# Two neighbouring transformer blocks on one core: a later place for two position tables, and a deeper ring for the first pass over the MLP weights

## The chip, the cores and the metric

The kernel runs on one core of one Trainium2 chip. The time is device microseconds (us) of the program, as the median of several runs. Five engines take their instructions in order, each from a queue of its own: PE (matrix products), DVE (vector), ACT (scalar functions), POOL (GpSimd) and SP, which here only issues DMA transfers. They wait for each other through semaphores. What decides the time is how long PE, which has nearly all the work, stands idle or runs at a lower granted clock.

## The reference

A sequence of 32 x 64 rows of 512 numbers goes through two blocks. Cut to what matters:

```python
# block 0: rotary attention with 8 heads over one key/value head, then a gated MLP
h = x * rsqrt(mean(x**2) + 1e-6) * (w * (1 + t @ tw.T))
q, k, v = h @ Wq.T, h @ Wk.T, h @ Wv.T           # 8 heads of 64, one k and v
q, k = rope(q, pos_ids), rope(k, pos_ids)        # cos and sin of pos * inv_freq
x = x + softmax(q k^T / 8) v @ Wo.T
h = ada_rms(x)                                   # second weights
x = x + (silu(h @ Wg.T) * (h @ Wu.T)) @ Wd.T     # 512 -> 2048 -> 512
# block 1: LayerNorm with scale and shift from t, keys and values through a latent of 128
h = layernorm(x) * (1 + scale) + shift
k, v = (h @ Wkd.T) @ Wku.T, (h @ Wkd.T) @ Wvu.T  # 16 heads, 4 k/v heads, rope
x = x + softmax(mask(q k^T / sqrt(32))) v @ Wo.T
```

The positions are an input, so the cosines and sines of block 0 are computed on the chip; that is what `angles` does.

## The kernel before, in words

All arithmetic is in 32-bit floats. The 2048 rows are cut into eight units of 256 (`NU`, `UT`). `attention0(u)` is the first block's attention of a unit, `attention1(u)` the second block's, and `mlp(j)` the first block's MLP for a block of units: `BLOCKS = ((0,), (1, 2), (3, 4), (5, 6), (7,))`, so mlp(0) is the MLP of unit 0, mlp(1) that of units 1 and 2, and so on. Each `mlp(j)` is one pass over all MLP weights.

**The order of the work.** PE's order is written by a planner at build time: jobs (the MLP pass, the attention of the units that the next pass needs, the second block's attention of units that are done) are generators that yield costs, and class `Order` (L74) takes the next piece from the job that is least advanced. The stretch before mlp(0), the prelude, has its order written out by hand in `FIRST`, with unit 0's attention ("a"), unit 1's ("b") and the four modulations ("m"). While mlp(0) runs (about 61 to 178 us), unit 2's attention is worked in; during mlp(1), units 3 and 4; during mlp(2), units 5 and 6; during mlp(3), unit 7 (`in_turn`, L1277). The other engines' queues follow from the order in which the code issues their instructions and from the build's own ordering of what has no dependence.

**The angles.** `angles(u0)` (L410 to L452) computes the cosines and sines for the two units u0 and u0 + 1 at once: 35 DVE instructions on 128 x 128 tiles (a cast L423; sign and size L424 to L427; splitting L428 to L430; products L438, rounding L433 and L434, sums L444 to L446) and two Sin on ACT (L450, L451), with a last DVE product L452. It is called through the argument `late` at the end of an `attention0`. `angles(2)` is called in the prelude and runs from 99 to 122 us. `angles(4)` is called at the end of unit 2's attention and `angles(6)` at the end of unit 4's. Who reads the result is the first step of an `attention0`: `tab` (L491), eight matmuls that turn the tables into the layout of q and k, from which DVE makes `cs` (L500). Unit 4's tab stands at 278.4 us and unit 6's at 527.9.

**The weights.** A pass has 24 weight sets: three matrices (gate, up, down) by eight groups q of 256 columns. In a pass they come as two halves of four groups, each eight gate and up sets and then four down sets. A product is done with seven block products in place of eight (P1 to P7): EARLIER (P1, P6, P5, P7) reads the f part of a set, four tiles, and LATER (P2, P3, P4) reads the l part, three tiles. Four of the seven tiles are sums of quarters of the matrix. In the first pass the four raw quarters of a set are loaded (two to l, one to f, one to a tile `a`, here called a21), and `sums_of_set` (L325) makes the sums: L330, L331, L332 on DVE (on POOL for sets 0 and 1), L333 on POOL. The sums are stored to memory (`kept`) by `done_with`, and the later passes load them ready made.

**The ring.** The sets live in `MW = 4` slots of each kind. When PE is done with a part of set n, `done_with` (L335) issues the load of set n + 4: in the first pass, all of it at once, when the l part is done (`load_sets`, L304); later each part by itself (`load_part`, L288). The a21 tile has two buffers (L310). `combine` (L317) issues the sums up to two sets ahead of PE's use; for sets 2 to 4 they are held back behind a mark in DVE's queue (L322), so that they don't stand ahead of the prelude's work. `other_mods` (L1187) loads sets 2 and 3 after the second modulation.

**The elementwise part of the MLP.** ACT copies a product out (e, L1059), DVE adds (L1060, L1061, L1080, L1089, L1098), ACT does silu (L1092), POOL the gating (L1100 to L1103), and PE takes the down products (`gu` and `down` both at L1044). In attention, DVE turns q (L631 to L633), takes the softmax's maximum, difference, sum and reciprocal (L643, L644, L651, L652), POOL scales (p, L653), PE transposes (pp, L658), ACT copies (pT, L659), and DVE adds the result (po) to x at L679.

Of the kernel before, what the change touches and what calls it, by code (L numbers as in the profile page):

```python
# [17 lines left out]
P = 128  # L18
# [5 lines left out]
NU = T // UT  # L24
HT = UT // 2
FF = 2048
NP = FF // P // 2
# [103 lines left out]
def two_blocks(ctx: ExitStack, tc: tile.TileContext, a: dict, out: bass.AP):  # L131
# [44 lines left out]
    def fixed(shape):  # L176
        n, i = int(np.prod(shape[1:])), stays["at"]
        stays["at"] += n
        assert stays["at"] <= STAY
        t = stays["all"][:, i : i + n]  # L180
        if len(shape) == 2:
            return t
        names = "abc"[: len(shape) - 1]
        return t.rearrange(f"p ({' '.join(names)}) -> p {' '.join(names)}", **dict(zip(names, shape[1:])))

    def work(tag, shape, name, bufs=2):
        return wk.tile(shape, F32, tag=tag, name=name, bufs=bufs)
# [81 lines left out]
        x_units[u] = xt  # L269


    MW = 4
    EARLIER = ("P1", "P6", "P5", "P7")
    LATER = ("P2", "P3", "P4")
    OF = {"P1": ("f", 3, "B11"), "P6": ("f", 1, "T2"), "P5": ("f", 0, "T1"), "P7": ("f", 2, "T3")}
# [7 lines left out]
    sets, odd = {"f": {}, "l": {}}, {}  # L283

    slots = {kind: [fixed([P, parts, 2 * P]) for i in range(MW)] for kind, parts in (("f", 4), ("l", 3))}
    act_slots = [fixed([P, 7, 2 * HT]) for i in GROUPS[0]]

    def load_part(kind, n):  # L288
        if n >= len(sequence) or n in sets[kind]:
            return  # L290
        j, m, q = sequence[n]
        i = 3 * q + m
        t = slots[kind][n % MW]
        if kind == "f":
            nc.sync.dma_start(t[:, 3], a["wmlp"][i][:, 0])
            if j:
                nc.sync.dma_start(t[:, 0:3], kept[i][:, 0:3])
        else:
            nc.sync.dma_start(t[:, 0:2], a["wmlp"][i][:, 1:3])
            if j:  # L300
                nc.sync.dma_start(t[:, 2], kept[i][:, 3])
        sets[kind][n] = t

    def load_sets(upto):  # L304
        for n in range(upto):
            if n in odd:
                continue
            load_part("f", n)
            load_part("l", n)
            odd[n] = work("a21", [P, 2 * P], f"a21_{n}", 2)  # L310
            nc.sync.dma_start(odd[n], a["wmlp"][3 * sequence[n][2] + sequence[n][1]][:, 3])

    marks, roots = [], []
# [21 lines left out]
    def done_with(kind, what):  # L335
        n = place[what]
        j, m, q = what
        if j == 0:
            to = kept[3 * q + m]
            if kind == "l":  # L340
                nc.sync.dma_start(to[:, 3], sets["l"][n][:, 2])
            else:
                nc.sync.dma_start(to[:, 0:3], sets["f"][n][:, 0:3])
        if n + MW < 3 * NP:
            if kind == "l":
                load_sets(n + MW + 1)
        else:
            load_part(kind, n + MW)

    mods = []  # L350

# [835 lines left out]
    def other_mods():  # L1187
        for i in range(1, 4):
            yield from modulation(i)
            if i == 1:  # L1190
                load_sets(MW)

    def second(u, room=None):
        room = room or {"ring": "1"}
# [11 lines left out]
    for _ in modulation(0):  # L1206
        pass
    load_positions(2)
    load_sets(2)
    load_mod(2)  # L1210
    load_mod(3)
# [7 lines left out]
    ahead = Job(attention0(1, {"ring": "1", "lean": True}, late=later_angles), A0)  # L1219
# [57 lines left out]
    def in_turn(units):  # L1277
        for u in units:
            while u not in x_units or u not in turned_units:
                yield 0.0, 1.0  # L1280
            late = (lambda u=u: angles(u + 2)) if u % 2 == 0 and u + 2 < NU else None
            yield from attention0(u, {"ring": "0"}, late=late)

    chain = Job(behind(), 0.8 * A1)
    for j, units in enumerate(BLOCKS):
# [5 lines left out]
        if j + 1 < len(BLOCKS):  # L1291
            more = [u for u in BLOCKS[j + 1] if u > 1]
# [112 lines left out]
```

## Time and profile before

| what | value |
| --- | --- |
| median of 3 runs | 1021.75 us (1021.2 to 1022.19) |
| profiled execution | 1023.49 us, span 1021.7 us |
| PE busy | 987.5 us, 97% of the span |
| DVE, ACT, POOL busy | 543.4, 302.9, 423.1 us |
| PE busy from 50 to 200 us | 136.1 of 150 us |
| DVE busy from 100 to 150 us | 43.97 of 50 us |
| mean granted clock of PE | 0.992 |

The profile is one execution; its parts are the engines' busy times, the span in 40 slices, the chain of waits that ended last, groups of instructions by line, and the DMA transfers. In a row of the timeline stand the start, the length, the engine, the line, the operation with output and inputs, and in brackets the idle time before it and what ended it. PE's idle time is what a change of order can win or lose: an engine that is not the bound may be idle for nothing. A PE instruction that waits on DVE or POOL has everything behind it in PE's queue waiting too.

### The profile page before, as it was taken

Reading aid. Unit: us, or ns where it says so; the run is one execution under the profiler, and the core shown is the slowest. Engines: PE = TensorE matmul, PEld = TensorE weight load, DVE = VectorE, ACT = ScalarE, POOL = GpSimd, SP = SyncE. Lnnn points to the kernel's source line nnn. Section 1 sums busy time; section 2 is a strip of 40 time slices with the busy share of each in tenths; the row PEclk is TensorE's granted clock in tenths of the full one; section 3 lists DMA queues with packets and bytes.
Section 4 is the critical chain, followed back from the end, with each engine's and each line's share of the span. In section 5 each row is a group of like instructions: output and inputs, shape, how many; then the busy total and the mean of one; then the engine's idle time right before and its main releaser. Section 6 shows DMA issues by size and latency. Waiting matters only on the chain.

```text
span 1021.7 us, 17480 instructions
## 1 busy us (share of the span) xinstructions
PE 987.5 (97%) x6710; PEld 857.6 (84%) x6710; DVE 543.4 (53%) x1188; ACT 302.9 (30%) x552; POOL 423.1 (41%) x439
## 2 busy tenths in 40 slices
PE   8999897999999999999999999999999989999998
PEld 7788887988877888888788887888788868998986
DVE  4757898654386442644446362455424632645274
ACT  4433142323215310225313351222313320425032
POOL 4336255354522433444344333554325432853252
PEclk9999998999999999999999999999999999999999
DMA  7927753724222345323242233333233424847301
GB/s 265 320 95 250 228 165 123 242 62 138 76 68 73 108 134 181 109 72 105 78 129 78 73 119 125 123 104 109 84 99 113 124 93 139 261 145 223 101 2 42
DMA packets 82642, 132.23 MB, mean 129 GB/s; under 512 B 8832, under 2 KB 48512, under 8 KB 82176
## 3 DMA queue, kind: packets, MB, share of 16 engines
q1 hardware_dynamic: 82560, 131.12, 40.1%
q8 instruction: 53, 0.87, 0.4%
q14 instruction: 29, 0.24, 0.1%
HBM read 114.31 MB, written 16.78 MB: 128 GB/s over the span
## 4 chain that ended last, share of the span: by engine, by line
PE 84%; DVE 8%; POOL 2%; DMA 2%; issue 2%; ACT 1%; POOLq 0%; SPq 0%; DVEq 0%; ACTq 0%
PE gu L1044 36%; PE down L1044 16%; PE q L623 11%; PE po L623 10%; PE sc L973 2%; PE pp L658 2%; PE kv L623 1%; PE lat L623 1%; PE cx L1003 1%; DMA stays<-in_wmlp 1%; PE cx L802 1%; ACT cT L812 1%; PE sc L781 1%; PE tab L491 1%; DVE mx L643 1%
## 5 line engine op out<-in xcount | busy, mean ns | idle before, releaser
L1044 PE MATMUL gu<-h,stays 128*128 128x256 f32 (+1 forms) x1280 | 261.2, 342 | 9.6 <-ACT gate L1092 5.8
L1044 PEld LDWEIGHTS gu<-h,stays 128*128 128x128 f32 x1280 | 208.4, 192 | 35.2 <-ACT gate L1092 6.0
L1044 PE MATMUL down<-stays 128*128 128x256 f32 (+1 forms) x1120 | 211.6, 344 | 2.0 <-DVE u_d L1060 2.0
L1044 PEld LDWEIGHTS down<-stays 128*128 128x128 f32 x1120 | 180.0, 194 | 25.9 <-issue 5.2
L1044 PE MATMUL gu<-hc,stays 128*128 128x256 f32 (+1 forms) x960 | 195.6, 339 | 0.5 <-DVE stays L331 0.5
L1044 PEld LDWEIGHTS gu<-hc,stays 128*128 128x128 f32 x960 | 157.9, 192 | 16.0 <-DVE stays L331 0.6
L623 PE MATMUL q<-h,stays 128*128 128x256 f32 x480 | 109.5, 381 | 0.0
L623 PE MATMUL po<-cT,stays 128*128 128x256 f32 x480 | 107.7, 381 | 0.9 <-ACT cT L812 0.7
L623 PEld LDWEIGHTS po<-cT,stays 128*128 128x128 f32 x480 | 90.4, 190 | 13.9 <-ACT cT L812 1.8
L623 PEld LDWEIGHTS q<-h,stays 128*128 128x128 f32 x480 | 90.6, 191 | 11.9 <-issue 0.2
L1100 POOL TENSOR_TENSOR stays<-gate,stays 128x768 f32<-128x768 f32 (+1 forms) x40 | 53.5, 1337 | 109.3 <-DVE stays L1089 102.4
L1059 ACT COPY e<-gu 128x256 f32<-128x256 f32 (+1 forms) x80 | 26.1, 326 | 193.9 <-PE gu L1044 193.8
L653 POOL TENSOR_TENSOR p<-p,sm 128x512 f32<-128x512 f32 x40 | 41.5, 1055 | 93.6 <-DVE sm L652 90.1
L634 POOL TENSOR_TENSOR qT<-u_q,v_q 128x512 f32<-128x512 f32 x30 | 38.1, 1268 | 90.0 <-DVE v_q L633 83.4
L679 DVE TENSOR_TENSOR x<-x,po 128x512 f32<-128x512 f32 x28 | 19.2, 687 | 99.2 <-PE po L623 99.2
L1060 DVE TENSOR_TENSOR u<-e,gu 128x256 f32<-128x256 f32 (+1 forms) x80 | 28.7, 360 | 61.1 <-ACT e L1059 61.1
L610 POOL TENSOR_TENSOR h<-x,stays 128x1024 f32<-128x1024 f32 x12 | 23.0, 1916 | 68.9 <-DVE x L679 51.2
L1061 DVE TENSOR_TENSOR w<-u,gu 128x256 f32<-128x256 f32 (+1 forms) x80 | 29.2, 365 | 30.9 <-PE gu L1044 30.0
L1101 POOL TENSOR_TENSOR stays<-stays 128x512 f32<-128x512 f32 (+1 forms) x40 | 43.8, 1096 | 2.7 <-DVE posf L423 0.2
L565 DVE RECIPROCAL stays<-stays 128x256 f32<-128x256 f32 (+1 forms) x23 | 35.4, 1540 | 16.9 <-ACT stays L564 16.8
L1147 POOL TENSOR_TENSOR x<-x,c 128x256 f32<-128x256 f32 x16 | 12.0, 749 | 74.8 <-DVE c L1134 74.8
L643 DVE TENSOR_REDUCE mx<-sc 128x8 f32<-128x512 f32 (+1 forms) x52 | 31.4, 641 | 17.6 <-PE sc L973 15.3
(233 smaller groups left out, 1281.9 us busy)
## 6 DMA issues: line engine op xcount, KB each, us to landing
stays<-sums SPq DMA_DIRECT2D x96, 384.0 KB, 3.1
stays<-in_wmlp SPq DMA_DIRECT2D x120, 256.0 KB, 3.1
stays<-in_wmlp SPq DMA_DIRECT2D x120, 128.0 KB, 2.6
stays<-sums SPq DMA_DIRECT2D x96, 128.0 KB, 2.4
sums<-stays SPq DMA_DIRECT2D x24, 384.0 KB, 3.7
mod<-in_mod SPq DMA_DIRECT2D x8, 512.0 KB, 5.4
x<-in_x SPq DMA_DIRECT2D x8, 512.0 KB, 5.6
a<-in_wmlp SPq DMA_DIRECT2D x24, 128.0 KB, 3.4
```

What stands on the lines that cost most here:

```text
L565: nc.vector.reciprocal(r, r)
L610: nc.gpsimd.tensor_tensor(by_seq(h), by_seq(x), per_seq(s, u), ALU.mult)
L623: nc.tensor.matmul(ps, w[:, k, cols], h[:, k, :], start=(k == 0), stop=(k == KC - 1))
L634: nc.gpsimd.tensor_tensor(dst, u, v, ALU.add)
L643: nc.vector.tensor_reduce(mx, s3, AX.X, ALU.max)
L653: nc.gpsimd.tensor_tensor(p8, p8, sm.unsqueeze(2).to_broadcast(wide), ALU.mult)
L1044: nc.tensor.matmul(ps[REGION[p]][:, c], w[:, slot, cols], moving, start=opening and ps.opens(p, c, k), stop=p in LATER, skip_group_check=True,
L1059: nc.scalar.copy(e, ps[0])
L1060: nc.vector.tensor_tensor(u2, e, ps[1], ALU.add)
L1061: nc.vector.tensor_tensor(w2, u2, ps[2], ALU.add)
L1100: e.tensor_tensor(act[:, 2:5], gate[:, 1:4], act[:, 2:5], ALU.mult)
L1101: e.tensor_tensor(act[:, 0:4:2], act[:, 2:4], act[:, 1:3], ALU.subtract)
```

## The change

Two things are changed, and nothing of the arithmetic.

1. `FIRST_MW = 6`: in the first pass the ring has six slots. The two extra slots (`more`) are tiles of the working pool. A set's load is issued when the set six before it is done. The a21 tile gets four buffers. `other_mods` loads sets 2 to 5 after the second modulation. In the first pass the slots of the sets 22 and 23 are not loaded again, and the second pass's first four sets are loaded when sets 18 to 21 are done. From the second pass on the ring has four slots, as before.
2. `late` now belongs to the odd units: unit 3's attention ends with `angles(4)` and unit 5's with `angles(6)`. So angles(4) moves from mlp(0) to mlp(1), directly ahead of unit 4's attention, and angles(6) from mlp(1) to mlp(2), directly ahead of unit 6's. `angles(2)` stays.

```diff
-    MW = 4
+    MW, FIRST_MW = 4, 6
...
     slots = {kind: [fixed([P, parts, 2 * P]) for i in range(MW)] for kind, parts in (("f", 4), ("l", 3))}
+    for i in range(FIRST_MW - MW):
+        t = work("more", [P, 7, 2 * P], f"more_{i}", FIRST_MW - MW)
+        slots["f"].append(t[:, 0:4])
+        slots["l"].append(t[:, 4:7])
...
-        t = slots[kind][n % MW]
+        t = slots[kind][n % (MW if j else FIRST_MW)]
...
-            odd[n] = work("a21", [P, 2 * P], f"a21_{n}", 2)
+            odd[n] = work("a21", [P, 2 * P], f"a21_{n}", 4)
...
-        if n + MW < 3 * NP:
+        ahead = n + (MW if j else FIRST_MW)
+        if ahead < 3 * NP:
             if kind == "l":
-                load_sets(n + MW + 1)
-        else:
-            load_part(kind, n + MW)
+                load_sets(ahead + 1)
+        elif j or n < 3 * NP - FIRST_MW + MW:
+            load_part(kind, ahead)
...
             if i == 1:
-                load_sets(MW)
+                load_sets(FIRST_MW)
...
-            late = (lambda u=u: angles(u + 2)) if u % 2 == 0 and u + 2 < NU else None
+            late = (lambda u=u: angles(u + 1)) if u % 2 and u + 1 < NU else None
```

In the order of PE's queue this moves a few matmuls of mlp(0), and in mlp(1) it puts 28 down products ahead of unit 4's tab that stood behind it; from there on PE's order is the same as before. On DVE the instructions of the two angles move with their calls, and set 5's sums stand in the prelude.

## The prediction

> **What bounds the kernel now.** I read the page's first two parts, then PE's busy time by stretches, then the list of what PE waited for, and last the timeline of two gaps.
>
> The page: busy time per engine, and the clock granted to PE in 40 slices.
>
> ```profile
> span 1021.7 us, 17480 instructions
> PE 987.5 (97%) x6710; PEld 857.6 (84%) x6710; DVE 543.4 (53%) x1188; ACT 302.9 (30%) x552; POOL 423.1 (41%) x439
> ...
> PEclk9999998999999999999999999999999999999999
> ```
>
> PE is the bound. The change leaves its matmuls alone, so all it can win or lose is PE's 34 us of idle time and the stretches at a lower clock. Where they lie shows in the busy time by stretches (us; then PE, PEld, DVE, ACT, POOL busy; granted clock, DMA share, GB/s):
>
> ```profile
> 50.00:100.00 50.00, 46.67 (x439) 42.79 (x438) 31.10 (x81) 18.20 (x38) 22.61 (x29) 1.00 0.53 178
> 100.00:150.00 50.00, 45.27 (x386) 41.16 (x385) 43.97 (x118) 14.06 (x26) 20.31 (x26) 0.97 0.59 191
> 150.00:200.00 50.00, 44.16 (x288) 41.54 (x287) 36.71 (x82) 13.78 (x25) 22.64 (x26) 0.93 0.59 193
> 200.00:250.00 50.00, 50.00 (x293) 43.65 (x292) 28.58 (x58) 13.62 (x22) 23.70 (x19) 1.00 0.32 99
> ...
> 300.00:400.00 100.00, 96.97 (x515) 81.75 (x510) 49.93 (x100) 25.91 (x45) 34.29 (x32) 1.00 0.38 120
> 400.00:500.00 100.00, 99.98 (x613) 85.13 (x611) 51.70 (x102) 33.64 (x55) 49.18 (x45) 1.00 0.32 97
> ```
>
> Some 14 us are idle between 50 and 200 us, which is the first pass over the weights (mlp(0), about 61 to 178 us). 3 us are idle in the second pass (300 to 400), nothing in the third (400 to 500). What ended PE's waits from 60 to 210 us (total, times, longest):
>
> ```profile
> PE gu L1044 <- ACT gate L1092: 5.8, 1, 5.8
> PE down L1044 <- DVE u_d L1060: 2.0, 1, 2.0
> PE gu L1044 <- issue: 1.2, 2, 0.9
> PE gu L1044 <- ACT sq_a L597: 1.0, 1, 1.0
> ```
>
> The 5.8 us gap is one event. The timeline of its makers (start, length, [idle before]):
>
> ```profile
> 165.28 1.97 DVE L434 TENSOR_TENSOR stays<-stays 128x128 f32<-128x128 f32 x1
> ...
> 167.82 0.92 DVE L452 TENSOR_TENSOR stays<-stays,sign 128x128 f32<-128x128 f32 x1
> 168.66 1.48 DVE L330 TENSOR_TENSOR stays<-a,stays 128x256 f32<-128x256 f32 x1
> ...
> 171.76 0.29 DVE L1080 TENSOR_TENSOR stays<-w,gu 128x128 f32<-128x128 f32 x1
> ```
> ```profile
> 172.15 2.05 PE L1044 MATMUL gu<-h,stays 128*128 128x128 f32 x8 [5.84 <-ACT gate L1092]
> ```
>
> The last up products of group 7 wait for L1080 on DVE, which stands behind the last of angles(4) (L423 to L452, 15.5 us of DVE from 135 to 169 us) and two sums of weights. The eight matmuls then take 2.05 us, where the same eight at 159.63 took 1.05: the granted clock was 0.50 from 172 to 175 us.
>
> In the second pass angles(6) does the same on a smaller scale:
>
> ```profile
> 308.55 1.12 PE L1003 MATMUL cx<-pT,stays 64*32 64x256 f32 x16 [2.57 <-ACT pT L659]
> ```
>
> **The change, part by part** (in the profiled execution of before: 1023.49 us, span 1021.7, 1.8 outside it; it lies 1.7 above the median 1021.75, and I take the sum off either).
>
> *angles(4) leaves mlp(0).* 35 DVE instructions and two Sin. L1080 then needs e (L1059), which needs sq_b and sq_a on ACT (1.06 and 1.04) after the second L679. Unit 2's po ends at 159.6, L679 is free to run by 160.3 instead of 164.42, so e ends near 162.8 and the four DVE steps to L1080 (0.27, 0.27, 0.41, 0.29) near 164.1; with one sum stretched like the 1.48 row, 165.6. PE wants it at 166.3. The gap goes: -5.84. With it goes the half clock: 8 gu 2.05 against 1.05, 4 hc 1.06 against 0.61, 16 down 3.10 against 2.21, together -2.3. **-8.1**; bounds: -4 if a stretched step uses up the slack and half of the gap stays without the half clock coming off, -8.1 at most.
>
> *Ring of six, a21 of four.* Loads start two sets earlier. PE's waits in 88 to 97 us (0.89 and 0.99) follow DVE waiting on loads of weights (DVE waits of 2.67, 1.31 and smaller ones between 70 and 95 us, about 7 us in all): **-1.8** (0 to -2.1). From 98 to 124 us DVE is 24.7 of 26 us busy with angles(2) (13.0 us) and sums; angles(2) stays, and the same number of sums stands in the queue, only of later sets. The 2.02 us wait and its clock loss (31 downs in 5.46 us; 109 to 112 us at 0.50; about 1.8 us) therefore stay: **-0.5** (0 to -5.0, if 2.02, 0.45, 0.77 and 1.8 all went). From 124 to 150 us three gaps of 0.35, 0.38 and 0.53: **-0.7** (0 to -1.3).
>
> *Set 5 in the prelude.* `combine` holds back sets 2 to 4 alone, so two of set 5's DVE sums (L330, L332) now stand in DVE's queue between unit 0's softmax subtractions (L644) and its L651, which started at 33.40 us without a wait. Set 5's loads are fourth and later on SP behind set 4's f part, which waits for PE's transposed modulation (ends 30.07) and POOL's qT (29.5). With 0.45 each on SP, a_5 is issued at 31.5 and f_5 at 32.0. Landing by the page (3.4 for a, 2.6 for 128 KB) 34.9, by what the same kinds took from 24 to 34 us (4.8, 4.6) 36.5. Two sums add about 1.0, so L651 starts 2.5 to 4.1 late, and behind it L652, POOL's p (35.12) and PE's pp at 36.38, which came without idle; PE's q at 36.82 stands behind pp. The loads of mod 3 (L359, 29.46) now go out behind set 5's, so the queues are emptier at 31: the low end. **+2.5** (0, if loads are early, to +5.9: 4.1 and a clock loss of 1.8 as after the 2.02 gap).
>
> *SP.* 554 transfers before and after. mod 3 goes out about 3 us later (about 5 to land, read at 53.8 by L380), the l parts of sets 2 to 4 too (read after 61), wq1 behind x_2, which waits for PE to 43 us (read after 61). 0 (to +1). Sets 24 to 27 start when 18 to 21 are done, not 20 to 23, so earlier; PE waits for no weights near 178 us now: 0.
>
> *angles(6) leaves mlp(1).* The gaps 0.34 (304.03) and 2.57 (308.55) lie where its 14.4 us of DVE alternate with unit 4's softmax. **-2.9** (0 to -2.9).
>
> *angles(4) enters mlp(1), ahead of unit 4's tab (L491).* 28 downs move ahead of that tab as cover: 28 x 0.43 = 12.0 us, so PE comes to it at 278.4 + 12.0 = 290.4 instead of 278.4. On DVE the angles start after unit 3's shuffle (L633, ends 273.2): 35 x 0.29 = 10.2, the reciprocals and h that stand there 1.75 + 1.23 + 1.75, u_d 0.40, the Sin pair and L452 0.9: 289.4. Uncontended it just fits; by the row of angles(6) beside POOL (14.4) it is 3.2 late. POOL is idle from 275.7 to 285.8, so nearer the low end; a hoisted down's later part also waits about 0.8 for its c22. **+2.0** (0 to +5).
>
> *angles(6) enters mlp(2)*, on DVE from 455.7 us, amid unit 5's softmax. 30 of its instructions (8.7 us) stand ahead of the L1080 that ended at 472.7, with L651 and L652 (1.6) now also ahead; DVE's idle time there is 4.9. So it ends at about 478.1, and PE needs it near 475.9: a gap of 2.2, beside 1.0 at 462.6 (L1089, same way). **+3.0** (0, as 458 to 478 has had no gap at all, to +6 by the stretched row 15.5).
>
> Each of these stretches is by POOL: L434 at 165.28 took 1.97 us, ending when POOL's h (165.18, 1.91 us) ended; the same step alone takes 0.29.
>
> Sum: -8.1 - 1.8 - 0.5 - 0.7 + 2.5 - 2.9 + 2.0 + 3.0 = **-6.5**: profiled 1017.0, median 1015.2.
>
> A rule that speaks against this: the Trainium skill, "TensorE: Matmul & The Clock Gate", Part 1: The HAM clock gate, says the clock is halved after an idle window of about 3.4 us that runs freely. Rows: 0.50 after the 2.02 and 5.84 gaps, 1.00 after the 2.57 one; so gap length alone doesn't decide here. By the rule alone the new gaps of 2 to 3 us would cost nothing further; by the 2.02 row each of the three new ones could cost 1.8 more, sum -1.1.
>
> **The rivals.**
> 1. *Slower: the prelude.* DVE takes its queue in order, so all of unit 0's softmax stands behind set 5's loads. For a longer wait speaks a DMA share of 0.94 to 1.04 from 32 to 40 us; against it, that set 5 is issued ahead of most of that traffic. Landing at 44 us, as wo0's 9.2 us plus 3 on SP would give, with a half clock after it: +12.4 in place of +2.5, sum +3.4, 1025.2. It decides from a price of 9 on (then the sum is 0).
> 2. *The cost only moves.* Both late angles stall PE as angles(4) did at 172: +5 and +8 in place of +2 and +3: +1.5, 1023.3. For it: one stands right ahead of a tab, the other in a softmax, where PE has had no slack to show. Against: DVE is 52% busy in 400 to 500, 73% in 150 to 200. One of the two alone: about 1019.
> 3. *More is freed.* Sums of later sets are done so early that the 2.02 gap goes, and mlp(2) hides all: -6.5 - 4.5 - 3.0 = -14.0, 1007.8. Against: DVE is full from 98 to 124 whatever was loaded.
> 4. *The ring does nothing*, since DVE and not the loads limits mlp(0): -6.5 + 3.0 = -3.5, 1018.3.
>
> **How the numbers follow.** A measurement tells 0.2% (2 us) from no change. Chances: forecast 0.46, rival 3 0.10, rival 4 0.12, one late angle dear 0.10, both dear 0.09 (0.05 of it over 1023.8, the rest within 2 us), prelude 0.13 (0.11 of it over 1023.8). Faster: 0.46 + 0.10 + 0.12 + 0.10 = 0.78; same 0.06; slower 0.16. The likeliest case's own range is 1011 to 1019 (terms about half way to their ends). For 8 in 10: from rival 3's 1007.8, less 0.8 for its ring gains, to 1023, short of the prelude's and the worst angles'.
>
> **What would show it.** No PE gap over 1 us at 160 to 175 us and clock 1.00 there. PE at 98 to 124 as now, 2.02 with 0.50 after it. DVE idle for a DMA near 33.4 us, and pp at 36.38 later with idle before it. An idle time under 3 us, ended by L452, ahead of unit 4's tab near 281 us (290 less 9); no gap at cx of unit 4's heads. Gaps of 1 and 2 us near 455 to 470, ended by DVE. Wrong if: the gap at 172 is only shorter, if angles in mlp(2) cost over 8 us, or if unit 0's softmax waits over 5 us for set 5.

## The result, and the profile after

The changed kernel takes 1029.26 us (median of 6 runs, 1026.87 to 1032.63); before takes 1022.08 in the runs beside it (6, 1021.2 to 1024.47). The ratio is 1.0069, interval 1.0047 to 1.0091: slower by 0.7%. The forecast, 1015.2 within 1007 to 1023, named the wrong side. The profiled execution of after took 1030.40 us, span 1028.6; that is 6.9 longer than before's span, where the sum of the steps said 6.5 shorter. So there are 13.4 us to explain.

The page of after, busy times and granted clock:

```profile
span 1028.6 us, 17480 instructions
PE 992.3 (96%) x6710; PEld 858.1 (83%) x6710; DVE 540.5 (53%) x1188; ACT 303.8 (30%) x553; POOL 423.8 (41%) x439
...
PEclk9999899999999999999999999999999999999999
```

The work is the same (6710 matmuls). PE's busy time is 4.8 us longer, and the mean granted clock 0.988 against 0.992. The dip in the clock has moved from slice 7 (153 to 179 us) to slice 5 (103 to 129 us). By stretches of after (length, then PE, PEld, DVE, ACT, POOL busy; granted clock, DMA share, GB/s):

```profile
25.00:50.00 25.00, 20.69 (x292) 16.49 (x282) 15.96 (x41) 9.69 (x23) 9.86 (x10) 0.93 0.74 236
50.00:100.00 50.00, 45.40 (x413) 41.11 (x413) 33.84 (x83) 18.68 (x38) 20.25 (x24) 1.00 0.70 239
100.00:150.00 50.00, 47.66 (x392) 44.54 (x392) 43.09 (x118) 12.98 (x24) 21.91 (x28) 0.93 0.60 196
150.00:200.00 50.00, 47.01 (x323) 43.56 (x322) 24.82 (x51) 16.18 (x27) 24.05 (x28) 0.97 0.50 165
...
400.00:500.00 100.00, 96.49 (x580) 81.06 (x580) 59.60 (x130) 30.37 (x51) 45.33 (x42) 0.98 0.29 88
```

From 150 to 200 us PE gained 2.9 us of work and DVE lost 11.9: angles(4) has left, as said. From 400 to 500 PE lost 3.5 and DVE got 7.9 more: angles(6) has come, and is not hidden. From 25 to 50 the clock is 0.93, where in before it was 1.00 and PE 22.75 us busy.

Landmarks in the trace cut the difference into sections. They are the first matmul of mlp(0), and the first matmul of the tabs of units 3, 5 and 6 (L496 in after; after's lines are four higher than before's at the sums of the weights, L330 to L333, and five higher from about L350 on). Lengths in us:

| section | before | after | change | the prediction's steps |
| --- | --- | --- | --- | --- |
| prelude, to mlp(0)'s first matmul | 61.2 | 64.8 | +3.7 | +2.5 |
| mlp(0), to unit 3's tab | 135.9 | 131.4 | -4.6 | -8.1 - 1.8 - 0.5 - 0.7 = -11.1 |
| mlp(1), to unit 5's tab | 219.3 | 220.9 | +1.6 | -2.9 + 2.0 = -0.9 |
| mlp(2), to unit 6's tab | 111.5 | 117.3 | +5.8 | +3.0 |
| the rest | 493.8 | 494.2 | +0.4 | 0 |

Every section came out worse than its step, so this is no single mishap. Half of the 13.4 us (6.5) is in mlp(0).

**The prelude.** The timeline of after, DVE and then PE:

```profile
35.19 0.43 DVE L334 TENSOR_TENSOR more<-a,more 128x256 f32<-128x256 f32 x1 [2.38 <-DMA a<-in_wmlp]
35.60 0.42 DVE L336 TENSOR_TENSOR more<-more,a 128x256 f32<-128x256 f32 x1
35.95 1.27 DVE L656 TENSOR_REDUCE sm<-p 128x8 f32<-128x512 f32 x2
...
38.70 0.65 PE L663 MATMUL pp<-stays,p 128*128 128x128 f32 x4 [2.83 <-POOL p L658]
39.19 5.31 PE L628 MATMUL q<-h,stays 128*128 128x256 f32 x16
```

Set 5's two sums wait for its load and hold up the softmax's sum (L651 before, L656 now) by 2.55 us, and pp by 2.3. The load landed just before 35.2, inside the 34.9 to 36.5 given. Then comes what the sum left out: the 16 matmuls of q take 5.31 us where in before they took 3.62, at half clock.

**mlp(0) at 100 us.** The timeline of after:

```profile
99.17 0.77 DVE L334 TENSOR_TENSOR more<-a,more 128x256 f32<-128x256 f32 x1 [0.26 <-DMA more<-in_wmlp]
99.86 0.28 DVE L1085 TENSOR_TENSOR stays<-w,gu 128x128 f32<-128x128 f32 x1
...
100.24 1.13 PE L1049 MATMUL gu<-h,stays 128*128 128x128 f32 x8 [2.76 <-issue]
```

The list of waits puts this down to "issue". In the rows PE's later up products of group 3 start 0.1 us after L1085 has ended. L1085 stands in DVE's order directly behind a sum of set 11, which waits for its load. In before the sum that stood ahead of it (L330 at 94.34) was of set 9. So the deeper ring didn't let DVE run further ahead of its loads. A set's load is now issued two sets earlier, but the build also placed its sums two sets earlier in DVE's order, and DVE waits for loads as it did before, in front of the same product. Ahead of that gap DVE waits 1.25 us for a load at 96.10, too.

**mlp(0) at 172 us.** The gap is 2.46 us in place of 5.84, and its cause is a new one. The timeline of after, ACT, POOL and PE:

```profile
168.09 0.91 POOL L558 TENSOR_TENSOR stays<-sq_b 128x256 f32<-128x256 f32 x1
...
169.03 1.06 ACT L602 ACTIVATE sq_a<-x 128x1024 f32<-128x1024 f32 x1 [3.79 <-POOL stays L558]
170.00 0.25 ACT L1064 COPY e<-gu 128x128 f32<-128x128 f32 x1
...
171.87 1.13 PE L1049 MATMUL gu<-h,stays 128*128 128x128 f32 x8 [2.46 <-issue]
```

ACT's square sq_a (of unit 3's first norm) waits 3.79 us until POOL has read sq_b (of unit 2's second norm). The two have nothing in common but storage: in before they had two places (sq_a starts at 167.69 us there without idle, while POOL reads sq_b until 171.6), and in after, with the two extra slots and two more a21 buffers in the working pool, one. Behind sq_a on ACT stands e (L1064), which DVE and then PE wait for. The prediction let e end near 162.8; it ended at 170.25.

**mlp(1) and mlp(2).** In mlp(1) the 2.57 us gap is gone, and there is no wait at unit 4's tab. Instead three waits stand at other places: 1.13 and 1.24 us at 282.26 and 285.06 (down products behind u_d and c on DVE, among angles(4)) and 0.97 at 328.25 (po, for ACT). In mlp(2), the timeline of after, PE and DVE:

```profile
477.95 1.13 PE L1049 MATMUL gu<-h,stays 128*128 128x256 f32 x4 [1.16 <-DVE u L1065]
480.86 2.08 PE L1049 MATMUL gu<-h,stays 128*128 128x256 f32 x4 [1.78 <-DVE stays L1085]
...
478.60 0.29 DVE L439 TENSOR_TENSOR stays<-stays 128x128 f32<-128x128 f32 x1
479.00 1.28 DVE L656 TENSOR_REDUCE sm<-p 128x8 f32<-128x512 f32 x2
480.20 0.32 DVE L657 RECIPROCAL sm<-sm 128x8 f32<-128x8 f32 x2
480.43 0.37 DVE L1085 TENSOR_TENSOR stays<-w,gu 128x256 f32<-128x256 f32 x1
```

Three gaps (0.55 at 464.05, and these two) make 3.5 us. They are the ones that the prediction described, down to the sum and reciprocal of the softmax ahead of the product.

**The clock.** Windows of 2 us in after, behind the gaps of the prelude, of 100 us and of mlp(2):

```profile
40.00:42.00 2.00, 2.00 (x7) 1.62 (x6) 1.77 (x5) 0.16 (x2) 1.56 (x2) 0.53 1.06 387
42.00:44.00 2.00, 2.00 (x7) 1.59 (x7) 0.00 (x0) 0.27 (x1) 0.00 (x0) 0.62 1.03 402
...
102.00:104.00 2.00, 1.92 (x9) 1.96 (x10) 0.41 (x1) 0.19 (x1) 1.92 (x3) 0.50 0.90 325
104.00:106.00 2.00, 2.00 (x11) 2.00 (x11) 1.88 (x5) 0.00 (x0) 0.88 (x2) 0.50 0.30 111
106.00:108.00 2.00, 2.00 (x12) 2.00 (x11) 1.97 (x6) 0.00 (x0) 1.84 (x4) 0.50 0.60 182
...
480.00:482.00 2.00, 1.14 (x3) 0.96 (x4) 1.97 (x6) 1.64 (x2) 1.47 (x2) 0.61 0.00 0
482.00:484.00 2.00, 2.00 (x7) 1.54 (x5) 1.97 (x5) 0.98 (x4) 0.57 (x1) 0.54 0.02 5
```

What a stretch loses is its length times one minus its clock. Behind the prelude's gap that is 2 x (0.47 + 0.38) = 1.70 us; behind mlp(2)'s, 2 x (0.39 + 0.46) = 1.70; from 172 to 178 us (0.81, 0.50, 0.84) 1.70; from 100 to 110 us (0.89, 0.50, 0.50, 0.50, 0.91) 3.40, which is twice as much. In before the stretch behind its 2.02 us gap (0.74, 0.50, 0.90) lost 1.72. So the loss comes in portions of 1.7 us. In before, half clock also stands at the 5.84 us gap, from 170.4 to 177.3 us in the trace's clock records, which is two portions (the prediction read it as 172 to 175 us); in the first 1.7 us of that stretch PE is still idle.

### The profile page after: what moved, and what is told of

It reads as the page before. It is cut to its first block, busy times and chain, and to the rows that moved or that the text cites. A ratio compares the mean times of both kernels' runs of the same rounds, so it can differ in the third digit from the quotient of the medians.

```text
span 1028.6 us, 17480 instructions
## 1 busy us (share of the span) xinstructions
PE 992.3 (96%) x6710; PEld 858.1 (83%) x6710; DVE 540.5 (53%) x1188; ACT 303.8 (30%) x553; POOL 423.8 (41%) x439
## 4 chain that ended last, share of the span: by engine, by line
PE 78%; DVE 9%; POOL 4%; ACT 3%; issue 2%; DMA 2%; SPq 1%; POOLq 0%; ACTq 0%; DVEq 0%
PE gu L1049 32%; PE down L1049 16%; PE q L628 10%; PE po L628 9%; PE sc L978 2%; PE pp L663 1%; PE lat L628 1%; PE cx L1008 1%; DVE sm L656 1%; PE kv L628 1%; ACT cT L817 1%; POOL p L658 1%; DMA more<-in_wmlp 1%; DVE mx L648 1%; PE cx L807 1%
## 5 line engine op out<-in xcount | busy, mean ns | idle before, releaser
L1049 PE MATMUL gu<-h,stays 128*128 128x256 f32 (+1 forms) x1216 | 252.1, 344 | 10.0 <-issue 5.2
L1049 PEld LDWEIGHTS gu<-h,stays 128*128 128x128 f32 x1216 | 199.5, 191 | 35.9 <-issue 10.7
L1049 PE MATMUL down<-stays 128*128 128x256 f32 (+1 forms) x1008 | 199.1, 352 | 3.1 <-DVE u_d L1065 1.8
L1049 PEld LDWEIGHTS down<-stays 128*128 128x128 f32 x1008 | 167.9, 195 | 27.7 <-issue 5.1
L1049 PE MATMUL gu<-hc,stays 128*128 128x256 f32 (+1 forms) x912 | 190.0, 342 | 0.6 <-DVE gate L1094 0.6
L1049 PEld LDWEIGHTS gu<-hc,stays 128*128 128x128 f32 x912 | 151.3, 191 | 17.2 <-DVE gate L1094 1.0
L628 PE MATMUL q<-h,stays 128*128 128x256 f32 x480 | 111.5, 385 | 0.0
L1064 ACT COPY e<-gu 128x256 f32<-128x256 f32 (+1 forms) x80 | 26.1, 327 | 188.6 <-PE gu L1049 188.3
```

Source lines behind the costliest of these rows:

```text
L628: nc.tensor.matmul(ps, w[:, k, cols], h[:, k, :], start=(k == 0), stop=(k == KC - 1))
L1049: nc.tensor.matmul(ps[REGION[p]][:, c], w[:, slot, cols], moving, start=opening and ps.opens(p, c, k), stop=p in LATER, skip_group_check=True,
L1064: nc.scalar.copy(e, ps[0])
```

## The experiments

Each ratio is to the kernel before on the same chip, in the same group of runs. Section lengths from the profiled executions, cut as above (us):

| kernel | median | ratio, interval | prelude | mlp(0) | mlp(1) | mlp(2) |
| --- | --- | --- | --- | --- | --- | --- |
| before | 1022.08 | | 61.2 | 135.9 | 219.3 | 111.5 |
| after | 1029.26 | 1.0069 [1.0047, 1.0091] | 64.8 | 131.4 | 220.9 | 117.3 |
| e1 ring only | 1032.01 | 1.0093 [1.0078, 1.0108] | 65.6 | 137.6 | 221.0 | 111.6 |
| e2 angles only | 1024.66 | 1.0021 [1.0008, 1.0034] | 60.7 | 130.0 | 219.3 | 118.8 |
| e3 set 5 held back | 1025.32 | 1.0029 [1.0015, 1.0042] | 60.4 | 132.0 | 220.9 | 118.8 |
| e6 angles(4) only | 1018.93 | 0.9956 [0.994, 0.9972] | 60.2 | 133.1 | 219.4 | 111.6 |
| e7 angles(6) only | 1023.26 | 1.0002 [0.9989, 1.0015] | 61.1 | 135.8 | 214.5 | 116.9 |
| e12 squares apart | 1026.96 | 1.0043 [1.0028, 1.0059] | 65.6 | 128.9 | 220.9 | 117.0 |
| e9 angles in pieces, old ring | 1019.12 | 0.9964 [0.9948, 0.998] | 60.4 | 130.9 | 217.4 | 114.4 |
| e13 ring mended, angles in pieces | 1015.33 | 0.9933 [0.9913, 0.9953] | 60.4 | 128.7 | 215.6 | 114.3 |
| e14 angles(2) in pieces too, old ring | 1018.32 | 0.9961 [0.9941, 0.998] | 61.2 | 130.3 | 215.3 | 114.4 |
| e15 the same with the mended ring | 1013.97 | 0.992 [0.9897, 0.9943] | 60.3 | 127.9 | 215.3 | 114.3 |

### Which half costs: e1 to e4

The first question was whether the ring by itself costs time (theory A) or does not (theory B). e1 is the change without the moved angles:

```diff
-            late = (lambda u=u: angles(u + 1)) if u % 2 and u + 1 < NU else None
+            late = (lambda u=u: angles(u + 2)) if u % 2 == 0 and u + 2 < NU else None
```

> The ring of six and the four a21 tiles, with the angles where they were before. Theory A (the ring costs: set 5's sums stall unit 0's softmax, and DVE stands on loads of later sets in mlp(0)): the prelude is 3 to 4 us longer, unit 2's tab 4 to 5 us later, and the gap at 172 us with its half clock stays: 1026 to 1028 us. Rival B (the ring gains as predicted, the moved angles cost): 1.5 to 3 us faster than before, about 1020.

Measured 1032.01, ratio 1.0093. The ring alone is 0.9% slower than before, so B falls. (Its interval overlaps that of after, so nothing follows on which of the two is slower.) The prelude is 4.4 us longer, with gaps of 3.03 us at 39.64 and 2.80 at 100.84; the gap at the end of mlp(0), here at 178.41, is 6.48 us, no shorter than in before.

e2 is the other half: the kernel before with the new line for `late` alone.

> Only the angles are moved, ring of four. Theory A: the gap of 5.8 us at 172 and its half clock (2.3) go whole, mlp(1) costs about 1.6 net and mlp(2) about 5.8 as in the changed kernel: 1021 to 1022 us. Rival C (what is left of the gap at 172 in the changed kernel comes from the angles' move and not from the ring): a gap of 2 to 3 us stays at 172, and the time is 1023 to 1025.

Measured 1024.66, ratio 1.0021. mlp(0) is 5.9 us shorter, mlp(1) is as long as before, and mlp(2) is 7.3 longer. So the moved angles come out slower too, by a little, and what they lose they lose in mlp(2). In mlp(0) the gap of 5.84 is gone, but one of 2.03 has come at 174.03, behind a sum (L331). Its set's first sum (L330, 172.79) waited 4.26 us for the load: on the ring of four, loads hold PE at the end of mlp(0) once angles(4) is out of the way.

e3 is after with set 5's sums held back like those of sets 2 to 4:

```diff
-            with after(tc, mybir.EngineType.DVE, marks[0]) if 2 <= n < 5 else nullcontext():
+            with after(tc, mybir.EngineType.DVE, marks[0]) if 2 <= n < 6 else nullcontext():
```

> The changed kernel with set 5's sums held back behind the mark like those of sets 2 to 4. Theory A: the 2.8 us gap before unit 0's pp and the half clock after it go: 3.5 us less than the changed kernel, about 1025.8. Rival D (the prelude waits for something else, or set 5 then stalls the first sets of mlp(0)): less than 1 us gained, 1028.5 or more.

Measured 1025.32: 3.9 us below after. The prelude is 4.5 us shorter, and 0.8 shorter than before's. The wait of mlp(0) stays: 3.49 us at 97.08, again directly behind L1085 and a sum of set 11 that waited 0.97 for its load. So the step "set 5 in the prelude" had the right mechanism.

e4 is before with the room of the extra slots taken by two tiles that nothing uses:

```diff
+    held = [work("more", [P, 8, 2 * P], f"more_{i}", 2) for i in range(2)]
+    for t in held:
+        nc.gpsimd.memset(t[:, 0, 0:1], 0.0)
...
+        if j == 0:
+            for held_tile in held:
+                nc.gpsimd.memset(held_tile[:, 0, 0:1], 0.0)
```

> The kernel before, with 16 KB of each partition's working memory held by two unused tiles until mlp(0) is done, as much as the ring's two sets and two a21 tiles take. Theory E (the ring's room makes working tiles share storage, and that adds waits): 1 to 3 us slower, 1023 to 1025, with PE gaps in mlp(0) that the kernel before has not. Rival (storage is not short): within 0.5 us of before.

Measured 1022.43, ratio 1.0003 [0.999, 1.0016]. Taking room is not enough to cost anything. In this kernel the two squares kept their two places (sq_a starts at 165.65 us without idle), so room alone doesn't make them share either; e12 is on the sharing.

### Where the late angles go: e6, e7, e5

e6 moves only angles(4), e7 only angles(6), both with the ring of four:

```diff
+            late = (lambda: angles(4)) if u == 3 else (lambda: angles(6)) if u == 4 else None
...
+            late = (lambda: angles(4)) if u == 2 else (lambda: angles(6)) if u == 5 else None
```

> Ring of four; angles(4) alone is moved to the end of unit 3's attention, angles(6) stays at the end of unit 4's. Theory A: mlp(0) 5.4 us shorter as with both moved, mlp(1) 2 us longer, mlp(2) as before: about 1019.5. Rival (the loss of mlp(2) comes with angles(4), through a shifted order): mlp(2) still 5 to 7 us longer, 1025.

Measured 1018.93, ratio 0.9956: faster, 0.6 from what was expected. That the number came out is in part luck. mlp(0) is only 2.8 us shorter and not 5.4, since a gap of 1.98 us stands at 174.92 with a portion of half clock behind it, and there, too, a sum had waited (4.21 us) for its load. In return mlp(1) is no longer for the 2 us that were expected. Three waits of 0.79, 1.24 and 1.03 us stand in it, but the 2.57 us gap of angles(6) doesn't come.

> Ring of four; angles(6) alone is moved to the end of unit 5's attention. Theory A: the 172 us gap stays, mlp(1) 2.9 us shorter, mlp(2) about 7 us longer (gaps of 0.6, 1.2 and 1.8 us and a half clock behind them): about 1027. Rival as for the run with angles(4) alone: mlp(2) unharmed, about 1020.

Measured 1023.26, no change (expected 1027). The gap at 172 stays at 5.83. mlp(1) is 4.8 us shorter, more than the 2.9 of the step, and mlp(2) 5.4 longer, more than its 3.0. The two parts of this move cancel.

e5 tries another place: each of the two angles in one run at the start of unit 3's or unit 5's attention, when DVE is less busy, and pinned there in DVE's order (ring of four):

```diff
+            if u % 2 and u + 1 < NU:
+                with after(tc, mybir.EngineType.DVE, latest(tc, mybir.EngineType.DVE)):
+                    angles(u + 1)
+            yield from attention0(u, {"ring": "0"})
```

> Ring of four; the two angles are moved one MLP later too, but to the start of unit 3's and unit 5's turn (and not before what DVE was given last), where DVE is about half busy and no softmax or tab waits. Theory A (where the angles land on DVE decides, not the number of instructions): the gap at 172 goes (5.4 us gained in the kernel with only the angles moved), the 2.9 us of mlp(1) go, and mlp(2) has no new gap: 8 us faster than before, about 1014.6. Rival (the 35 instructions cost the same wherever they stand): no better than the kernel with only the angles moved, 1022 or more.

Measured 1021.21, ratio 0.9982, far from the 1014.6 expected, and 0.8 short of the rival's 1022. The timeline of e5, DVE and PE:

```profile
204.26 0.68 DVE L631 TENSOR_TENSOR v_q<-q,cs 128x512 f32<-128x512 f32 x1
204.86 0.21 DVE L433 TENSOR_SCALAR stays<-stays 128x128 f32<-128x128 f32 x1
205.00 0.68 DVE L632 TENSOR_TENSOR u_q<-q,cs 128x512 f32<-128x512 f32 x1
...
207.79 0.69 DVE L745 TENSOR_TENSOR vT<-kv,stays 64x512 f32<-64x512 f32 x1
...
208.59 2.04 PE L1044 MATMUL gu<-h,stays 128*128 128x256 f32 x4 [3.23 <-issue]
```

Even in a stretch where DVE was about half busy in before (28.58 of 50 us from 200 to 250), 35 small instructions put down in one piece make a new gap of 3.23 us, with a portion of half clock behind it (0.57, 0.57 in the two windows from 208 to 212). They stand on DVE from 186.81 to 206.7 us, and unit 3's q and k, which come due meanwhile, alternate with them. PE's product starts 0.1 us after L745, the last of these that reads kv, has ended; the list of waits says "issue" here, so this is read from the times. In e9 below, with the angles in pieces, L745's counterpart starts at 203.73 and there is no such gap. A second gap of 2.00 stands at 426.77 and is put down to the same instruction. The mean busy share of DVE says nothing of this: what matters is how long a product for PE stands behind the angles.

### The sums in mlp(0): e8, e10, e11

If sums that come too early in DVE's order make the gap at 97 to 100 us, putting them later must take it away. e8 is e3 with each later set's sums pinned behind the latest instruction on DVE:

```diff
+            mark = marks[0] if n < 6 else latest(tc, mybir.EngineType.DVE)
+            with after(tc, mybir.EngineType.DVE, mark) if n > 1 else nullcontext():
```

> The changed kernel with set 5 held back and with each later set's sums kept behind what DVE was given last before them, so that the sums of sets 10 and 11 stand behind and not ahead of L1085 of up 3. Theory F (the ring's loads come earlier, but the sums were put earlier in DVE's queue by as much, and L1085 stands behind them): the 3.5 us gap at 97 us shrinks below 1 us, its half clock goes, 1021 to 1022.5. Rival (the loads themselves are late, or PE then waits for sums): 1025 or more.

Measured 1030.0, ratio 1.0066. The gap is gone, and from the start of mlp(0) to the row_b matmuls behind group 3's up products it took 33.0 us (35.8 in before, 37.3 in after, 39.1 in e3), with the same 288 matmuls in between. So the cause of that gap is confirmed, though the time is the rival's. For the planner now put unit 2's tab earlier (by 118 matmuls in the trace against e3, not the 58 of the next expectation), and there PE waited 8.57 us at 110.67 for L458, the last product of angles(2). e10 puts that tab back:

```diff
+            if u == 2:
+                yield 0.0, 12.0
+            with after(tc, mybir.EngineType.PE, latest(tc, mybir.EngineType.PE)) if u == 2 else nullcontext():
                 cos, sin = tables(u, r)
```

> The kernel with set 5 held and the sums kept later, with unit 2's tab back behind the down products of the first half, where the kernel before has it (its first matmul came 58 matmuls earlier there and waited 8.6 us). Theory F (sums too early on DVE made the gap at 97 us): that gap stays away and the 8.6 us go: 1020 to 1022. Rival (the sums put later only move the wait): 1025 or more.

Measured 1031.44, as the rival said: the wait moved rather than went. The timeline of e10, DVE and PE:

```profile
111.80 0.29 DVE L458 TENSOR_TENSOR stays<-stays,sign 128x128 f32<-128x128 f32 x1 [0.58 <-ACT stays L457]
112.01 0.42 DVE L335 TENSOR_TENSOR more<-a,more 128x256 f32<-128x256 f32 x1
...
112.48 3.78 PE L1053 MATMUL down<-stays,more 128*128 128x128 f32 x16 [8.84 <-DVE more L335]
```

Pinned, the sums of set 10 stand behind the whole of angles(2), and PE waits 8.84 us for them. The build's own place for the sums was too early by a load, and this one too late by an `angles`. e11 is e10 with angles(4) and angles(6) in pieces (as in e9, next):

> Both together: ring of six, set 5 held, sums later, tab of unit 2 in its old place, angles in pieces. If the ring gains once its sums no longer stand ahead of L1085: 2 to 4 us less than the kernel with the spread angles alone, 1011 to 1013. Rival (DVE limits mlp(0), and the ring has nothing to give): the same as that kernel, 1014 to 1016, or more.

Measured 1028.69, with the same 8.84 us wait: worse than the rival, too. Pinning all sums is no remedy.

### The angles in pieces: e9

The remedy that e5 points to is to cut the run. `angles` becomes a generator of nine pieces, which the planner deals out over the first third of mlp(1) and mlp(2), each pinned where it comes (ring of four):

```diff
+    def spread_angles(u0, cost):
+        pieces = angle_pieces(u0)
+        going = True
+        while going:
+            with after(tc, mybir.EngineType.DVE, latest(tc, mybir.EngineType.DVE)):
+                going = next(pieces, pieces) is not pieces
+            yield cost, 0.0
...
+        if j in (1, 2):
+            must.append(Job(spread_angles(2 * j + 2, 0.4), 12.0))
```

> Ring of four; angles(4) and angles(6) are cut into nine pieces of three to five DVE instructions, handed out over the first third of mlp(1) and of mlp(2), each kept behind what DVE was given last. Theory A (the loss is the unbroken or softmax-bound run of 35 instructions ahead of what PE waits for): 5.4 us gained in mlp(0), 2.9 in mlp(1), nothing lost in mlp(2): about 1014.5. Rival (the pieces still delay PE's partners on DVE): 1019 or more, no better than angles(4) alone.

Measured 1019.12, ratio 0.9964: 5.5 us better than the same angles in one run (e2), less than expected (1014.5). mlp(2) is 2.9 us longer than before, not 7.3. Small gaps remain: 0.97 and 0.97 near 248 us, 1.53 and 0.73 near 470. In mlp(0) the wait for a load has stayed (2.50 at 173.21). By its time the rival is met: e6, which moves angles(4) alone and in one piece, is no slower (1018.93). e6's places together with the deeper ring were not run.

### The shared storage: e12

If sq_a waits at 172 us only because it shares its place with sq_b (theory G), a place of its own takes the gap away. After, with unit 3's squares apart:

```diff
-... work("sq", [P, KC, UT], f"sq_{name}", 1)
+... work("sq3" if name == "a3" else "sq", [P, KC, UT], f"sq_{name}", 1)
```

> The changed kernel with unit 3's squares in a tile of their own. In the changed kernel unit 3's sq_a and unit 2's sq_b have the same storage, and sq_a waits for POOL to have read sq_b; e of up 7 stands behind it on ACT. Theory G: the 2.46 us gap at 172 goes, 1026.5 to 1027. Rival (that gap comes from the loads of set 23, or from POOL's order): 1029, gap still over 2 us.

Measured 1026.96, 2.3 below after. The timeline of e12, ACT and PE:

```profile
168.38 0.27 ACT L1064 COPY e<-gu 128x128 f32<-128x128 f32 x1 [1.29 <-PE gu L1049]
...
170.61 1.13 PE L1049 MATMUL gu<-h,stays 128*128 128x128 f32 x8 [0.49 <-issue]
```

e now waits for PE's product and not for POOL. The gap of 2.46 is 0.49, and the clock behind it is 1.00, so the portion of 1.7 us went with it. G holds by the trace (the two ratios' intervals, of e12 and of after, overlap). With a place of its own sq_a doesn't only stop waiting: the build puts it at 54.40 us on ACT, far ahead of e. In mlp(1) of after the next pair shows the same wait (2.88 us at 271.67, none in before), and no run with the ring of six takes that one away. mlp(0) is 2.5 us shorter, where 2.0 of gap and 1.7 of clock make 3.7: the wait at 100 us is 3.8 us in this kernel, 1.0 more.

### All together: e13 to e15

e13 is after with set 5 held back (e3), the squares apart (e12) and the angles in pieces (e9).

> The changed kernel with all three causes found so far taken out together: set 5 held (4.0 us by itself), unit 3's squares in a tile of their own (2.3 by itself), the late angles in pieces (5.5 between the kernels with only the angles moved). If they are the causes and add up: 1029.3 - 4.0 - 2.3 - 5.5 = 1017.5. If they are one wait seen three times, or the ring costs something else too: 1021 or more.

Measured 1015.33, ratio 0.9933; the causes add up, and a little more (1017.5 was expected). What PE still waits for in e13 from 60 to 200 us:

```profile
PE gu L1065 <- issue: 3.7, 2, 3.2
PE down L1065 <- DVE u_d L1081: 1.8, 1, 1.8
PE gu L1065 <- DVE stays L1101: 1.0, 1, 1.0
```

The first is mostly the wait at 97 us again (3.2), the second is before's 2.02, still behind angles(2). e14 takes on that one: angles(2) in pieces as well, spread over mlp(0), with the ring of four (theory H: this frees it at no other cost).

```diff
-        if j in (1, 2):
+        if j in (0, 1, 2):
```

> The kernel with spread angles on the ring of four, and angles(2) in pieces as well, over the start of mlp(0), in place of 13 us in one run at 98 to 124 us. Theory H (DVE full with angles(2) is what holds PE at 98 to 124, with either ring): the 2.0 us gap with its half clock and the 0.8 go: 1014 to 1016. Rival (DVE there waits for loads and sums, not for time): 1019 or more.

Measured 1018.32, against 1019.12 of e9, so H as stated falls. The 2.02 gap is gone, but others stand in its place: 1.87 at 96.06, 1.24 at 101.58, 1.93 at 131.11, and 3.37 at 164.76 with half clock behind it. The last one's makers in e14, DVE and PE:

```profile
163.97 0.50 DVE L330 TENSOR_TENSOR stays<-a,stays 128x256 f32<-128x256 f32 x1 [3.39 <-DMA stays<-in_wmlp]
164.39 0.27 DVE L1096 TENSOR_TENSOR stays<-w,gu 128x128 f32<-128x128 f32 x1
...
164.76 2.04 PE L1060 MATMUL gu<-h,stays 128*128 128x128 f32 x8 [3.37 <-issue]
```

PE starts 0.1 us after L1096, and L1096 stands behind a sum that waited 3.39 us for its load. So here, with the ring of four, a load is what PE waits for. e15 is the same with the ring of six, set 5 held back and the squares apart:

> The same with the ring of six, set 5 held and unit 3's squares apart. If loads limit the first half of mlp(0) once angles(2) is out of the way, the ring shows its gain here: 2 us or more below the same kernel on the ring of four. If DVE's time limits it: the same within 1.5 us, or slower.

Measured 1013.97, ratio 0.992 [0.9897, 0.9943], the fastest of all: 8.3 us below before and 15.3 below after. Its page:

```profile
span 1012.1 us, 17474 instructions
PE 980.6 (97%) x6710; PEld 849.8 (84%) x6710; DVE 557.0 (55%) x1188; ACT 302.3 (30%) x552; POOL 426.1 (42%) x439
```

PE's busy time is 6.9 us below before's for the same matmuls, nearly all of it by the clock (mean 0.998 against 0.992, which is 6 us of the span). The sums ahead of the last up products wait at most 0.84 us for a load, and the gap of 3.37 is gone. The pairs with and without the ring now give its worth, set 5's hold and the squares' own place included: 1015.33 against 1019.12 (e13, e9) and 1013.97 against 1018.32 (e15, e14), that is 3.8 and 4.4 us. By ratios, 0.9933 against 0.9964 and 0.992 against 0.9961; each pair's intervals overlap a little, and both pairs point the same way. e14 and e15 ran side by side, and each of e15's four runs (1013.73 to 1015.01) is below each of e14's six (1016.95 to 1021.28).

## Why the prediction was wrong, step by step

**Angles(4) leaves mlp(0), -8.1: right for the cause that it named, wrong for the section.** e2 and e6 show that the gap of 5.84 goes with the angles: mlp(0) is 5.9 and 2.8 us shorter. But in after e ended at 170.25 and not near 162.8, since sq_a ahead of it shared a place with sq_b, which it does only with the ring (e1 shows the same wait, 3.84 us, and e2 none). The step counted "e then needs sq_b and sq_a on ACT (1.06 and 1.04)" and did not ask what those two wait for. The new gap cost 2.46, with 1.7 of clock behind it; e12 shows that the sharing is its cause. This wait was not in any rival. On the ring of four the step falls short, too: in the gap's place came the wait of 2 us for a load at 174 us (e2, e6, e9), where the prediction had "PE waits for no weights near 178 us now: 0". So the ring's gain lies there, once angles(4) has left, and not only at 88 to 97 us, where the prediction had put it.

**The ring, -1.8 - 0.5 - 0.7 = -3.0 in mlp(0): the wrong sign.** In after the ring made mlp(0) longer (131.4 against 130.0 in e2). The failed step is "Loads start two sets earlier ... -1.8". It took DVE's waits for loads as fixed in place, so that earlier loads would end them. The build moved the sums earlier together with the loads, and DVE waited in front of L1085 as before: gaps of 0.89 and 0.99 became one of 2.76 with two portions of clock loss (3.4; why two, no run shows). e8, with the sums later, shows the cause of the gap. Rival 4 ("the ring does nothing, since DVE and not the loads limits mlp(0)") is wrong too: with its side effects mended the ring is worth about 4 us (e13, e15). That is near the 3.0 of the step, but not by the step's path.

**Set 5 in the prelude, +2.5: right mechanism, too small.** The wait (2.38) and the delay of pp (2.3) are as worked out. The portion of half clock, which the step had put into its upper end (+1.8) and not into the sum, came: 2.3 + 1.7 = 4.0, measured +3.7, and 3.9 in the median by e3.

**angles(6) leaves mlp(1), -2.9, and angles(4) enters it, +2.0.** The gap of 2.57 went. The +2.0 was expected ahead of unit 4's tab; there was no wait there, but 1.13 and 1.24 at down products whose u_d and c stood among the angles (a hoisted down's wait was put at 0.8), and 0.97 at po. PE's idle time in the section is 3.71 us against 3.13. Another 1.0 is in PE's busy time, with as many records (1228 in both); I have not placed it. The failed step is that the two were added: on the ring of four, mlp(1) takes 219.3 us with angles(6) alone (before), 219.3 with angles(4) alone (e2), 219.4 with both (e6) and 214.5 with neither (e7). So the first of them costs 4.8 and the second nothing, and exchanging one for the other is worth 0, not -0.9. The +1.6 of after stands in the kernels with the ring alone (220.9 to 221.0 in e1, e3 and e12); its cause stays open.

**angles(6) enters mlp(2), +3.0: right gaps, too low a price.** 0.55 + 1.16 + 1.78 = 3.5 against 1.0 + 2.2 = 3.2, at the places named, ended by DVE. A portion of 1.7 stands behind the last, but it doesn't make up the rest: in e7 and e12 the same gaps were followed by full clock, and mlp(2) was still 5.4 and 5.5 longer than before. There PE waited at the cx that follows instead (in e7 its 16 matmuls stand from 477.11 to 479.05 us, in before they took 1.09). With two portions (e2, e3) it was 7.3 longer.

**The clock is the term that was mis-sized throughout.** The prediction set 1.8 for each of three new gaps beside the sum, by before's row of the 2.02 us gap, and then left it out. By the rule of the Trainium skill that it named beside it ("TensorE: Matmul & The Clock Gate", Part 1: The HAM clock gate) these gaps would have cost nothing further; the measurement decides against that. In after, portions came behind the prelude's gap (1.7), the one at 100 us (3.4, where 1.8 was kept from before), the one at 172 us (1.7, where none was kept) and mlp(2)'s (1.7): 1.7 + 1.6 + 1.7 + 1.7 = 6.7 us above the sum, half of the 13.4 missed, if each counts in full; by e7 and e12 the last one mostly doesn't. The rest is idle time: the gap of 2.46 at 172, the larger one at 100, and the smaller misses of mlp(1) and mlp(2).

Rival 2 ("both late angles stall PE", 1023.3) was right for angles(6) and wrong for angles(4), and rival 1 had the right place but too long a landing. No case joined the prelude's cost with the angles'. Taking each step at its likely value, when nearly every step had its bad end on the same side (a wait brings a clock loss, and no gap pays one back), made, in my reading, the range too low as a whole.

## What to carry to other kernels

A deeper ring had two side effects here that no diff shows: the build put the work on the new loads earlier into queues that other work stands in, and with the new buffers two tiles that had places of their own came to share one and waited for each other across engines (taking the same room by itself, e4, did not do that). Look at both in the built order, hold the new sets' sums back and give a tile on the critical chain its own place. A block of small instructions that was moved in one piece stalled whoever stood behind it even on a half busy engine; in pieces it cost less. Put the price of a new gap of 2 us or more at its length plus a portion of clock loss, and of two shorter ones close together as well. And a deeper ring pays where a wait for a load is what stands ahead of PE, so ask which waits will be left once the others are gone. The three remedies together turned +0.7% into -0.7% here.

## What the runs showed of the hardware that had not been expected

The granted clock falls to 0.50 for a fixed time. A portion cost 1.70 to 1.72 us: after's prelude, 172 and 480 us, before's 110 us, e3 at 96 to 102 us (0.85, 0.50, 0.79), e5 at 208 to 212; that is 3.4 us at half clock. Two in a row stand at 100 us in after (3.40) and at 170 us in before. That length agrees with the window of about 3.4 us that the Trainium skill gives ("TensorE: Matmul & The Clock Gate", Part 1: The HAM clock gate). But the idle time ahead of it was far below 3.4 us: 2.83, 2.76, 2.46 and 1.78 us in after, 2.02 in before. The 2.57 us gap in before was followed by 1.00, and so was the 1.24 us one at 285 us in after. Between 1.8 and 2.8 us the length of one gap did not decide.

What decided is where the idle time falls. In each of the 17 profiles, the stretches at half clock start whole steps of 3.413 us apart. In after they start at 40.10, 101.54, 173.22, 480.42 and 842.23 us, which are 18, 21, 90 and 106 steps. Cut into such steps, the idle time of PE in one step goes with the clock of the next. Counted over all profiles, behind steps at full clock: with 1.97 us idle or more, the next step was at 0.50 in 57 of 57 cases; with less than 1.8 us, in 1 of 4913; in between, in 3 of 8. Three pairs of steps, two of before and one of after:

```profile
105.57:108.98 3.41, 1.39 (x11) 1.25 (x11) 3.24 (x13) 1.03 (x2) 0.25 (x1) 1.00 0.66 199
108.98:112.39 3.41, 3.41 (x18) 3.41 (x18) 3.27 (x7) 0.00 (x0) 0.47 (x1) 0.50 0.22 48
...
307.00:310.41 3.41, 1.86 (x20) 1.14 (x21) 3.33 (x11) 2.63 (x6) 1.31 (x2) 1.00 0.01 2
310.41:313.82 3.41, 3.41 (x20) 3.00 (x19) 3.38 (x7) 0.96 (x3) 2.85 (x5) 1.00 0.40 125
...
477.01:480.42 3.41, 1.13 (x4) 0.68 (x4) 3.26 (x10) 3.35 (x5) 0.00 (x0) 1.00 0.33 91
480.42:483.83 3.41, 2.97 (x7) 2.44 (x8) 3.34 (x8) 2.03 (x5) 2.04 (x2) 0.50 0.00 0
```

The 2.02 us gap lies whole in one step and was followed by half clock. The 2.57 us gap is cut by a border: 1.55 us of it lie in the step shown, and the clock stayed full. In after, part of the 1.78 us gap and the 1.16 us one ahead of it make 2.28 us in one step. So the same gap can cost a portion in one execution and none in another: a gap of 2.77 us ahead of a pp (835.05 us in before) stands in all 17 profiles, and half clock followed it in eight.

The six runs of after lie 5.8 us apart (1026.87 to 1032.63), where those of e15, with few gaps, lie 1.3 apart in its group. In after the mean clock of a run goes with its time (0.993 for the fastest, 0.988 to 0.990 for the three slowest), which fits portions that come in one run and not in another; only the profiled executions show single portions, so that is not shown.
